# A Perceiver block on one core: VectorE and ScalarE in source order, with each step split in two

## Chip, cores and metric

The kernel runs on one core of a Trainium2 chip. The metric is the device time of one execution in microseconds (us); three runs of the kernel before are given, and one further execution was profiled. All arithmetic is in fp32.

The core's engines, as the profile names them: PE is TensorE (matrix multiplication; PEld is the loading of its stationary operand, which overlaps), DVE is VectorE, ACT is ScalarE, POOL is GpSimd, SP is the engine whose queue issues most of the DMAs. PE writes its products to PSUM, eight banks of 128 x 512 floats here; DVE and ACT read them from there.

## The reference

`x` is (4, 256, 256): four batches of 256 latents with 256 channels. `ctx` is (4, 4096, 192). Three residual stages follow each other, each on a normalised `x`:

```python
x = x + cross_attention(layernorm(x), ctx)     # 16 heads of 16, 4096 keys a batch
x = x + self_attention(layernorm(x))           # causal, 16 heads, q and k layernormed by head
x = x + slot_ffn(layernorm(x))
```

The slot network, for each batch, cut to its steps:

```python
h     = gelu(concat(x, slot_mean) @ w1 + b1)            # 256 x 128
logit = (h @ w2 + b2) / (abs(tau) + 0.1)                # 256 x 64 slots
alpha = softmax over the 8 largest logits, else 0       # routing
si    = (alpha.T @ x) / alpha.sum(tokens)               # slot inputs
gi, gh = si @ Wih.T + bih, S @ Whh.T + bhh
r, z  = sigmoid(i_r + h_r), sigmoid(i_z + h_z)
n     = tanh(i_n + r * h_n)
S_new = (1 - z) * n + z * S                             # gates
y     = S_new + attention among the 64 slots
out   = (alpha @ (layernorm(y) @ wvp + bvp)) @ wo + bo
```

## The kernel before

The function `fast_` (L914 to L1767) is what runs; an exact version stands behind a test on the softmax denominators (`in_range`, L1537, sets its condition) and isn't entered with these inputs.

**Rounds.** The cross-attention of a batch goes over its 4096 keys in 8 chunks of 512, and each chunk in two rounds, so there are 16 rounds `p` per batch `b`. The 8 PSUM banks are four pairs, `two[0]` to `two[3]`; a round calls them `w, x_, y, z` and the next round starts three pairs on. A round issues, in this order:

1. `cross_block` (L1617), the first of two: score matmuls (L183), 8 of them into each two pairs, and ScalarE's exps, two halves for the first pair (L1628) and whole pairs after (L1630);
2. `behind(w)`: the former round's `cross_weigh` (L1633), which multiplies its probabilities with the values (L197) into pair `w`; VectorE adds the result to the running sums (L1640, L1642), which frees the pair;
3. the second `cross_block`, into `x_, y, z, w`;
4. plan steps (below), into single banks of `x_` and `y`;
5. half of the next chunk's operands: keys in even rounds (`keys`, L92: matmuls L98 and L104, copies into `kt` by DVE L112 and ACT L113), values in odd ones (`values`, L119: matmuls L125 and L138, copies into `v` by DVE and ACT, L168). Each is split into `most()` and `rest()`, and the rest with the copies comes after the steps.

**Plan.** Everything behind the cross-attention of batch `b` is done as small steps in the rounds of batch `b+1`, from a table `plan[b, p, i]` (L1573 to L1607) with i = 0 or 2 ahead of the keys or values and 1 behind `most()`. In round 0 the sums are turned and divided (`cross_turn`, `turn` L207); round 1 projects (`cross_out`, L1248); rounds 2 to 4 make the self-attention's q, k and v (`qk`, L1266); an extra round 6 (`SELF_AT`) does its scores and exps (`self_block`, L1644) with the causal masks (L1668); round 7 turns the result, round 8 projects it (`self_out`, L1328); rounds 9 to 16 are the slot network: `hidden` (gelu, L1344), `routing` (L1349), `slot_inputs`, `gates` (L1419), `slot_qkv`, `slot_scores` (L1467), `at_turned` (L1478), `slot_mix` (L1483), `slot_values`, and `give` in round 5 of the batch after. The next batch's latents are loaded in round 2 (`load_x`, L993), normalised after round 8 (`normed_x`, L1003; `layernorm` L953), and made into queries in rounds 10 and 13. Weights that the steps share are made in the rounds of batch 0 by `set_...` functions.

After the fourth batch a fifth pass, b = 4, has only plan steps. To keep PE busy there, `fill` (L1044) issues idle matmuls at L1047, as many as the table `WAITS` gives in us, 0.43 us each.

**What sets the order.** PE is under a manual schedule in the main loop: it executes in source order. The order on DVE, ACT and POOL is chosen by the tile scheduler. Each engine executes its own instructions strictly in the order chosen, so an instruction that waits holds all behind it. Loads are issued by SP's queue, in order as well.

**Start.** The first latents are loaded, normalised and turned; the queries of batch 0 come first, then keys and values of chunk 0, then round 0.

## Time and profile before

| what | value |
|---|---|
| three runs | 934.31, 934.25, 930.0 us (median 934.25) |
| the profiled execution | 931.51 us, its span 929.7 us |
| ScalarE's large exps, L1630 | 384 times, 1045 ns each |
| score matmuls, L183 | 2048 instructions' worth in 282.8 us |
| weighing matmuls, L197 | 4096, 235.1 us |
| fill matmuls in the trace, L1047 | 162 records, 40.8 us |
| mean granted TensorE clock | 0.988 |

The page gives busy time by engine, the chain of work that ended last, and groups of instructions with their idle time and the operation that ended it (the "releaser"). A line of the timeline shows start, duration, engine, source line, operation, output and input, and in brackets how long the engine had been idle and who released it. "PEclk" is the share of the full clock that TensorE was granted. Matmul records can be missing to a few per cent, so counts in the page are below the program's.

Rounds without a step take some 10.5 us (batch 0: rounds begin at 50.94, 61.48 and 72.10), a batch from b = 1 on 17 rounds; the batches begin near 212, 425 and 640 us.

### The profile page before, as it was taken

The numbers are of one execution on the slowest core, as the hardware profiler recorded it, in microseconds if no ns is written. First come the engines' busy times: TensorE is split into PE (matmuls) and PEld (weight loads), VectorE is DVE, ScalarE is ACT, GpSimd is POOL, SyncE is SP. The second block draws the span as 40 slices with busy tenths as digits, with TensorE's granted clock in tenths as the row PEclk, the third lists the DMA queues.
The fourth block names the chain that finished last, engine by engine and source line by source line (L and its number), as shares of the span: only waits on it lengthen the run. The fifth ranks groups of instructions, "written<-read, shape, count | busy, mean of one in ns | idle before, by whom it ended". The sixth has DMA issues, their size and how long they took to land.

```text
span 929.7 us, 19031 instructions
## 1 busy us (share of the span) xinstructions
PE 880.1 (95%) x8171; PEld 471.4 (51%) x8171; DVE 331.1 (36%) x876; ACT 589.7 (63%) x833; POOL 45.1 (5%) x53
## 2 busy tenths in 40 slices
PE   8599999999999999999999999999999999999885
PEld 5244545544554545544554545545555455545563
DVE  5212222222444442322444243332344332224653
ACT  2477776757767677577666677667666777671320
POOL 1000100000002000000002010000001100000200
PEclk9799999999999999999999999999999999999997
DMA  6500101000000000000001000000001000000000
GB/s 181 136 24 24 35 24 47 24 24 24 23 24 24 24 5 20 24 24 24 24 24 35 2 24 24 24 24 24 24 23 36 2 24 24 1 2 1 12 1 17
DMA packets 21758, 25.72 MB, mean 28 GB/s; under 512 B 6496, under 2 KB 13216, under 8 KB 21664
## 3 DMA queue, kind: packets, MB, share of 16 engines
q1 hardware_dynamic: 20992, 23.88, 8.5%
q8 instruction: 66, 1.08, 0.5%
q10 hardware_dynamic: 576, 0.52, 0.2%
q14 instruction: 28, 0.23, 0.1%
q0 software_dynamic: 96, 0.01, 0.0%
HBM read 23.35 MB, written 1.05 MB: 26 GB/s over the span
## 4 chain that ended last, share of the span: by engine, by line
PE 84%; DVE 5%; ACT 5%; SPq 2%; DMA 2%; issue 1%; ACTq 0%; DVEq 0%
PE banks L183 28%; PE banks L197 25%; PE banks L990 6%; PE banks L98 6%; PE banks L125 5%; PE banks L104 3%; PE banks L138 3%; ACT prob L1630 3%; SPq L69 1%; PE banks L978 1%; PE banks L1682 1%; PE banks L1655 1%; PE banks L1047 1%; ACT prob L1665 1%; PE banks L212 1%
## 5 line engine op out<-in xcount | busy, mean ns | idle before, releaser
L1630 ACT ACTIVATE prob<-banks 128x1024 f32<-128x1024 f32 x384 | 367.5, 1045 | 12.0 <-PE banks L183 11.9
L183 PE MATMUL banks<-qh,kt 32*128 32x512 f32 x2048 | 282.8, 625 | 18.4 <-DVE kt L112 9.5
L197 PE MATMUL banks<-prob,v 128*32 128x256 f32 x4096 | 235.1, 381 | 3.9 <-ACT prob L1628 2.3
L1628 ACT ACTIVATE prob<-banks 128x512 f32<-128x512 f32 x256 | 139.0, 595 | 144.6 <-PE banks L183 144.4
L197 PEld LDWEIGHTS banks<-prob,v 128*32 128x32 f32 x4096 | 126.7, 110 | 129.6 <-ACT prob L1628 45.0
L183 PEld LDWEIGHTS banks<-qh,kt 32*128 32x128 f32 x2048 | 108.0, 184 | 146.3 <-issue 77.0
L1642 DVE TENSOR_TENSOR sums<-banks,sums 128x512 f32<-128x512 f32 x120 | 82.5, 691 | 215.0 <-PE banks L197 191.0
L125 PE MATMUL banks<-wv,ctx 128*128 128x256 f32 x256 | 62.5, 387 | 0.1
L98 PE MATMUL banks<-ctx,wk 128*128 128x512 f32 x128 | 61.7, 603 | 0.0
L125 PEld LDWEIGHTS banks<-wv,ctx 128*128 128x128 f32 x256 | 45.8, 190 | 13.0 <-ACT prob L1628 3.2
L113 ACT ACTIVATE kt<-banks,bk 128x512 f32<-128x512 f32 x32 | 22.0, 687 | 41.2 <-PE banks L104 41.0
L168 ACT COPY v<-banks 128x512 f32<-128x512 f32 x32 | 18.8, 587 | 45.1 <-PE banks L138 44.7
L1047 PE MATMUL banks<-idle 128*128 128x256 f32 x162 | 40.8, 398 | 2.9 <-DVE idle L1042 1.5
L112 DVE TENSOR_SCALAR kt<-banks,bk 128x512 f32<-128x512 f32 x32 | 24.0, 750 | 43.3 <-PE banks L104 42.9
L138 PE MATMUL banks<-wv,ctx 64*128 64x256 f32 x256 | 36.4, 401 | 0.0
L104 PE MATMUL banks<-ctx,wk 64*128 64x512 f32 x128 | 36.1, 641 | 0.0
L1665 ACT ACTIVATE prob<-banks 128x512 f32<-128x512 f32 (+1 forms) x40 | 23.9, 694 | 19.1 <-PE banks L1655 19.1
L168 DVE COPY v<-banks 128x512 f32<-128x512 f32 x32 | 21.9, 683 | 39.6 <-PE banks L138 39.6
L1047 PEld LDWEIGHTS banks<-idle 128*128 128x128 f32 x162 | 31.0, 199 | 8.6 <-ACT prob L1665 2.2
L1668 POOL TENSOR_TENSOR prob<-prob,tri 128x256 f32<-128x256 f32 x32 | 27.1, 866 | 166.1 <-ACT prob L1665 166.1
L98 PEld LDWEIGHTS banks<-ctx,wk 128*128 128x128 f32 x128 | 21.3, 190 | 19.3 <-ACT prob L1630 9.8
L1259 POOL TENSOR_TENSOR xo<-xo,abo 128x512 f32<-128x512 f32 x4 | 5.1, 1280 | 493.2 <-DVE tmp L965 493.2
(212 smaller groups left out, 578.8 us busy)
## 6 DMA issues: line engine op xcount, KB each, us to landing
ctx<-in_ctxT SPq DMA_DIRECT2D x32, 256.0 KB, 2.9
ctx<-in_ctxT SPq DMA_DIRECT2D x64, 128.0 KB, 3.1
x<-in_x SPq DMA_DIRECT2D x4, 256.0 KB, 3.9
out<-tmp SPq DMA_DIRECT2D x4, 256.0 KB, 2.5
wih<-in_ffn_WihT SPq DMA_DIRECT2D x1, 768.0 KB, 6.2
tmp<-in_ffn_WhhT SPq DMA_DIRECT2D x3, 256.0 KB, 4.7
wq<-in_L_xattn_Wq ACTq DMA_DIRECT2D x1, 256.0 KB, 4.1
wo<-in_L_xattn_Wo SPq DMA_DIRECT2D x1, 256.0 KB, 5.5
```

What stands on the lines that cost most here:

```text
L98: nc.tensor.matmul(pk[c], k.wk[:, 0, c * P : (c + 1) * P], cx[:, 0, :], start=True, stop=False)
L104: nc.tensor.matmul(pk[c], k.wk[left(c), 1, c * P : (c + 1) * P], cx[left(c), 1, :], start=False, stop=True,)
L125: nc.tensor.matmul(pv[n // 2][:, n % 2, :], cx[:, 0, n * P : (n + 1) * P], k.wv[:, 0, :], start=(n % 2 == 0), stop=False, skip_group_check ...
L138: nc.tensor.matmul(pv[u][:, i, :], cx[left(u), 1, n * P : (n + 1) * P], k.wv[left(u), 1, :], start=False, stop=True, skip_group_check=True,)
L168: copy(v[:, :, 0 : H * VW].rearrange("p i (h w) -> p i h w", w=VW)[:, :, :, 0:D], src.rearrange("p i (h d) -> p i h d", d=D),)
L183: nc.tensor.matmul(sc[:, m, :], kt[r, c, i * P : (i + 1) * P], qh[r, c, :], start=True, stop=True)
L197: nc.tensor.matmul(po[q * 32 : (q + 1) * 32, s * NQ : (s + 1) * NQ], v[:, i, w0 : w0 + 32], pr[s][:, m, e * NQ : (e + 1) * NQ], start=(fir ...
L990: nc.tensor.matmul(dst, lhs(c), rhs(c), start=(c == 0), stop=(c == 1))
L1047: nc.tensor.matmul(bank[:, 0:NQ], idle[:, 0:P], idle[:, 0:NQ], start=True, stop=True)
L1628: nc.scalar.activation(pt[:, m, :], sc[:, m, :], AF.Exp)
L1630: nc.scalar.activation(pt, sc, AF.Exp)
L1642: nc.vector.tensor_tensor(s.sums[c], po[:, c, :], s.sums[c], ALU.add)
```

## The change

- PE, DVE and ACT are put under the manual schedule, for the whole of `fast_`: each executes in source order. POOL and SP are as before.
- Steps become generators with one `yield`. What stands before it (it empties PSUM, as far as it can) runs at the step's place; what stands after runs once the round's `rest()`, with the `kt` or `v` copies, has been issued. Such a yield is put into `cross_out`, `qk`, `self_out`, `hidden`, `routing`, `gates`, `slot_scores` and `slot_values`.
- `load_x(1)` is issued right behind the second context chunk's load. The later loads stay in round 2 of the batch before.
- Start: keys' `most()` is issued before the queries, and the values of chunk 0 become the `behind` of round 0. The reduction `parity` and `pscale` come after the first layernorm.
- The two causal masks of a probability tile, one by POOL and one by DVE, become one DVE operation over both.
- `turn` takes the reciprocal straight from PSUM and copies the denominators after the multiplication. `gates` does the z part before the n part.
- Plan: `at_turned` moves from (14, 1) to (15, 0), `slot_mix` from (15, 2) to (16, 2), `slot_values` from (16, 0) to (5, 0) of the next batch, with `give` behind it at (5, 1). `in_range` is cut in two, at (9, 2) and (13, 1) of the last pass.
- `WAITS` and `SELF_WAIT` are lowered by eight fill matmuls in all.

```diff
-SELF_WAIT = 1.3
+SELF_WAIT = 0.86
 WAITS = {
-    0: (0.0, 1.3),
+    0: (0.0, 0.86),
...
-    6: (0.0, 3.0),
-    7: (0.0, 1.3),
+    6: (0.0, 2.2),
+    7: (0.0, 0.86),
...
-    12: (2.2, 0.0),
-    13: (0.4, 0.0),
-    14: (1.3, 0.0),
+    12: (1.7, 0.0),
+    13: (0.0, 0.0),
+    14: (0.86, 0.0),
...
-    nc.vector.tensor_copy(den, hd[:, :, :, D])
     rec = pool.tile([P, QT, 8], F32, name="rec", tag="rec")
-    nc.vector.reciprocal(rec, den)
+    nc.vector.reciprocal(rec, hd[:, :, :, D])
...
+    nc.vector.tensor_copy(den, hd[:, :, :, D])
...
-    with ExitStack() as es:
+    with ExitStack() as es, tc.manual_schedule(
+        engines={mybir.EngineType.PE, mybir.EngineType.DVE, mybir.EngineType.Activation}
+    ):
         return fast_(es, tc, nc, a, out, k, const, x0)
...
     cx1 = load_ctx(nc, a, cp, 0, 1)
+    batches[1].x = load_x(1)
...
         nc.vector.tensor_tensor(x1, halves(bank), s.xo, ALU.add)
+        yield
         s.x1n = halves(temp())
         layernorm(s.x1n, x1)
...
         nc.vector.tensor_tensor(s.x2, halves(bank), s.xo, ALU.add)
+        yield
         s.x2n = held.tile([P, QT, C], F32, name="x2n", tag="x2n", bufs=1)
         layernorm(s.x2n, s.x2)
...
         product(bank[:, 0:NQ], lambda c: w1[:, c, :], lambda c: s.x2nT[:, c, :])
+        yield
         s.hT = small.tile([DH, NQ], F32, name="hT", tag="hT", bufs=1)
         nc.scalar.activation(s.hT, bank[:, 0:NQ], AF.Gelu, bias=b1c)
...
+        yield
         for t in range(QT):
             nc.vector.max(best[:, t, :], lg[:, t, :])
...
-            ((14, 1), step(at_turned, s)),
-            ((15, 2), step(slot_mix, s)),
-            ((16, 0), step(slot_values, s)),
+            ((15, 0), step(at_turned, s)),
+            ((16, 2), step(slot_mix, s)),
...
-        plan[b + 2, 5, 0] = step(give, s)
-    plan[B, 13, 1] = in_range
+        plan[b + 2, 5, 0] = step(slot_values, s)
+        plan[b + 2, 5, 1] = step(give, s)
+    plan[B, 9, 2] = all_in_range
+    plan[B, 13, 1] = count_bad
...
-                for m in range(2):
-                    diag = pt[:, m, 0:n].rearrange("p (e q) -> p e q", e=2)[:, :, 0:P]
-                    (nc.vector if m else nc.gpsimd).tensor_tensor(
-                        diag, diag, tri.unsqueeze(1).to_broadcast([P, 2, P]), ALU.mult
-                    )
+                diag = pt[:, :, 0:n].rearrange("p m (e q) -> p m e q", e=2)[:, :, :, 0:P]
+                nc.vector.tensor_tensor(
+                    diag,
+                    diag,
+                    tri.unsqueeze(1).unsqueeze(1).to_broadcast([P, 2, 2, P]),
+                    ALU.mult,
+                )
...
+            def take(i, *room):
+                f = plan.get((b, p, i))
+                g = f and f(*room)
+                if g:
+                    next(g)
+                    late.append(g)
...
+            for g in late:
+                next(g, None)
```

## The prediction, before the result was known

> **What bounds the kernel now.** I read the page's busy shares first, then its chain of waits, then what TensorE waited for, then the stretches behind the long waits.

> ```profile
> PE 880.1 (95%) x8171; PEld 471.4 (51%) x8171; DVE 331.1 (36%) x876; ACT 589.7 (63%) x833; POOL 45.1 (5%) x53
> ...
> PE 84%; DVE 5%; ACT 5%; SPq 2%; DMA 2%; issue 1%; ACTq 0%; DVEq 0%
> ```

> TensorE is the bound. The change keeps its order and its count (but for eight fill matmuls), so it can win only from idle time of PE, the missing 5%, and from a lowered clock. The waits of PE by releaser:

> ```profile
> PE banks L183 <- DVE kt L112: 9.5, 1, 9.5
> PE banks L183 <- ACT prob L1665: 5.4, 3, 1.8
> PE banks L1479 <- DVE at L1476: 4.3, 3, 1.4
> PE banks L183 <- DVE v L168: 3.3, 5, 1.7
> ```

> One wait outweighs any other line; its stretch from the timeline (start, duration, what; in brackets the idle time before and who ended it), and then in 2 us windows (length, busy us of PE, PEld, DVE, ACT and POOL, granted clock, DMA share, GB/s):

> ```profile
> 32.04 0.59 SPq L995 DMA_DIRECT2D x<-in_x  x1
> 36.17 0.75 DVE L960 BATCH_NORM_STATS2 ln_st<-x 128x6 f32<-128x256 f32 x2 [7.67 <-DMA x<-in_x]
> 38.66 0.75 DVE L112 TENSOR_SCALAR kt<-banks,bk 128x512 f32<-128x512 f32 x1
> 39.46 2.09 PE L183 MATMUL banks<-qh,kt 32*128 32x512 f32 x8 [9.50 <-DVE kt L112]
> ```

> ```profile
> 30.00:32.00 2.00, 0.00 (x0) 0.00 (x0) 0.00 (x0) 1.98 (x3) 0.00 (x0) 1.00 0.46 46
> ...
> 40.00:42.00 2.00, 2.00 (x16) 0.29 (x12) 0.80 (x3) 0.39 (x1) 0.00 (x0) 0.50 0.00 0
> 42.00:44.00 2.00, 2.00 (x32) 0.98 (x28) 0.00 (x0) 1.55 (x2) 0.00 (x0) 0.71 0.00 0
> 44.00:46.00 2.00, 2.00 (x40) 0.97 (x36) 0.69 (x1) 0.00 (x0) 0.00 (x0) 1.00 0.00 0
> ```

> The scheduler put the layernorm of the second latents (L960) ahead of the key copy L112 on VectorE, and its data was issued at 32.04 and came at 36. So PE stood 9.5 us and then ran at half clock until 43.

> **The start: −13.** The load of x(1) moves ahead on SP's queue, behind the second context chunk; the layernorm goes to round 8. What is left in its place is the copy alone; next in PE's way there is the exp L1630 that it waited 0.33 for at 50.87. Round p=1 began at 28.82 and p=2 at 50.87: 22.05 us where the next rounds take 10.55 (61.48 less 50.94). That is 11.5 saved. The first key copy ran at 15.92 and 17.69 because queries (wq, then a wait on a weight) stood first; keys first and chunk 0's values in round 0 save about 1.5 more. −13, bounds −12 to −14: x(1)'s 256 KB now go ahead of the weights on SP's queue, and at the 265 GB/s seen at 32 to 34 that delays each by 1 us; the first reader of those, L1114's mean of wqkv, moves to p=4. If x(1) were late again, 11.5 is the price.

> **The rounds of a batch, three times (b=1 to 3).** In a round PE does scores, weighs the former round, more scores, plan steps, half of the next keys or values. A step's remainder now runs after the kt or v copies.
> - Gains. v copies behind statistics or a variance chain: L183 ×16 takes 2.4 for about 1.98 at p=1 and 3.48 for 1.95 at p=3, so −0.46 −1.45. at_turned goes a round later, off the wait at L1479: −1.4. Masks: 32 POOL and 32 VectorE operations (0.87 by the page, 0.56 to 0.72) become 32 VectorE ones of twice the width, 0.72 to 1.44; I take 1.1, twice 0.56. In the self round at 296 the last of POOL's ends at 299.41 (296.70+2.71), VectorE's at 298.82, and L1682 waits 0.76 for the former: −0.4. The longer mask runs beside ScalarE's exps L1665 (0.69); without that cover the last two a round would cost 2×0.4 more.
> - Hidden's gelu. Before, its table load came ahead of the copy:

> ```profile
> 545.76 1.28 ACT L1347 ACT_TABLE_LOAD   x1
> 547.41 0.47 ACT L1347 ACTIVATE hT<-banks,b1c 128x256 f32<-128x256 f32 x1 [0.36 <-PE banks L990]
> 548.50 0.69 ACT L113 ACTIVATE kt<-banks,bk 128x512 f32<-128x512 f32 x1 [0.62 <-PE banks L104]
> 549.21 1.28 ACT L1628 ACT_TABLE_LOAD   x1
> 550.50 1.09 ACT L1628 ACTIVATE prob<-banks 128x512 f32<-128x512 f32 x2
> 551.15 1.07 PE L197 MATMUL banks<-prob,v 128*32 128x256 f32 x16 [0.75 <-ACT prob L1628]
> ```

> Now: copy 0.69, load 1.28, gelu 0.47, load 1.28, then exps, which the weighing matmuls wait for: the first 1.28+0.47 come behind the copy, +1.75 and so +1.8 with a gap on PE of 0.75+1.75=2.5. Bounds 0 (the scheduler lifts the load) and 1.8; I take 1.8, nearest to the rows.
> - Routing. The six small activations L1376 (559.58 to 561.2) now follow the v copies and VectorE's top-8 chain, and still precede L1628's exps: the weighing begins 4.3 us after the scores for 2.87 before, +1.4, bounds 0 and 1.5.
> - Gates, z ahead of n: the matmul after it waits 0.2 to 0.5 longer: +0.5.
> - Sum of these: −0.46−1.45−1.4−0.4+1.8+1.4+0.5 = 0.0 a batch, bounds −3.2 and +0.5.

> **Two layernorms in a row.** At p=8 self_out's and the next batch's stand behind each other:

> ```profile
> 534.63 0.75 DVE L960 BATCH_NORM_STATS2 ln_st<-x 128x6 f32<-128x256 f32 x2
> ...
> 540.75 3.45 PE L183 MATMUL banks<-qh,kt 32*128 32x512 f32 x16
> 541.09 0.74 DVE L965 TENSOR_SCALAR tmp<-x,ln_mv,rs_y 128x256 f32<-128x256 f32 x2
> 541.74 1.28 DVE L1642 TENSOR_TENSOR sums<-banks,sums 128x512 f32<-128x512 f32 x2
> ```

> Interleaved they took 7.2 (534.63 to 541.83). One alone takes 4.1 to 4.3 (853.06 to 857.18 in the tail), two 8.6, and the v copies go ahead: the sums, which free the banks of the second block's scores, come 2.4 later in b=1 and b=2, with a gap on PE of up to 3.3. In b=3 there is no next batch: −0.5. Together +4.3, bounds −1.4 (only the copies gained) and +5.

> **The tail (b=4) and batch 0.** With no cross rounds PE runs fills and plan steps. Eight fills fewer save at most 8×0.43=3.4, and give back where the step behind them is late: VectorE's serial layernorm +0.2 twice, the second variance chain behind a copy +0.8, slot_values now in the last round +1.25, routing +0.3, against −1.4 in the self block and −0.6 in p=7 and p=14. With p=0's −0.3: about +0.6, bounds −3 and +3. Batch 0's set steps +0.5, bounds 0 and 1.

> **The sum without the clock.** −13 + 0.5 + 0.0 + 4.3 + 0.6 = −7.6.

> **The clock.** Gaps on PE lower it. In the self rounds PE waits 1.78 for L1665's exps, three times, and once the clock fell:

> ```profile
> 509.48 3.52 PE L183 MATMUL banks<-qh,kt 32*128 32x512 f32 x16 [1.79 <-ACT prob L1665]
> ```

> The window 510.78 to 514.19 had 0.50 granted: 3.41 us of half clock, work worth 1.7 lost, 1.65 with the edges. New gaps: gelu 2.5 and routing 2.2 three times each, p=9's up to 3.3 twice: eight. If each falls in the grid as its length over 3.41 (which makes the 1.78 gaps 0.52 each, one in three seen), that is 3×0.73+3×0.65+2×0.97 = 6, or +10. At the low end, gaps that are half as long as reckoned (they were added from durations in a row, with nothing of the preceding step let through), none. I take two windows, +3.3, since the row nearest in length, 1.78, cooled in one of three; bounds 0 and +13.

> [...]

> **The total.** −7.6+3.3=−4.3 on this execution's 931.5 (span 929.7) is 927.2. The runs' median, 934.25, lies 2.7 above it; I go some way towards it and say **928**.

> **Rivals.**
> 1. *The gaps cool the clock six or seven times* (+10 to +11 instead of +3.3): 931.5−7.6+10.5 = 934.4, no change. For it: the 1.79 gap that did it. Against: two of three like it didn't.
> 2. *The rounds win too.* If the gelu and routing remainders fall into slack (ScalarE is 63% busy, VectorE 36%), gelu and routing add nothing, the batches win 3.2×3=9.6 and p=8 wins 1.4: −13−9.6−1.4+0.5+0.6 = −22.9, so 908.6; midway to the forecast's −4.3, 918. Against: L1628's exps follow in order.
> 3. *Source order turns ScalarE into the gate of step rounds* (slower). ScalarE is not free to run exps while a remainder waits for VectorE; every round with a split remainder, seven a batch, 28 with the tail, would stand a further 0.7 beyond what I priced, the wait of L1628's releaser row (0.76), 28×0.7=20: 931.5−4.3+20 = 947. It decides from 0.42 a round (11.7 us, reaching 938.9). For it: ScalarE is the busiest engine beside PE. Against: most remainders are VectorE's alone.
> 4. *The start is not won*: x(1)'s load or the weights behind it delay chunk 1's work, and 8 of the 13 go: 936.

> **Chances.** About 0.5% (4.7 us) is what a measurement can tell from no change: faster is below 929.6, slower above 938.9. The forecast 0.45 (0.37 of it faster, 0.07 the same, 0.01 slower); the rounds win 0.17; cooled clock 0.15 (0.12 the same, 0.03 slower); start not won 0.04, the same; source order gates 0.19, slower. Faster 0.54, the same 0.23, slower 0.23. The forecast's own range is 921 to 934; with one in ten left on each side the range is 914 to 942.

> **What would show it.** The 9.5 wait at L183 gone and p=2 beginning near 38: the start right. L1347's load after L113, and L197 waiting 2.5 behind it: gelu right. L1642 at p=8 to 9 near 545, L183's ×16 over 5 there: layernorms right. Windows at 0.50 after these: the clock, counted at 1.65 each. A batch's period against 213.6 now (425 to 640, less the start) tells the rounds apart from the start. If the start's gain is under 10, or a batch's period moves over 4, the forecast is wrong.

## The result, and the profile after

Over twelve runs each, the kernel before has a median of 931.7 us (930.0 to 934.31) and the changed one 932.58 us (929.2 to 935.0). The ratio of the two is 1.0005, with a 95% interval of 0.9992 to 1.0018: no change that can be told from none. (The prediction's three runs had a median of 934.25; with twelve it lies at 931.7, and that is what the following differences are taken against.) The profiled execution after has a span of 931.7 us against 929.7.

The page after, first the busy times, then TensorE's granted clock in forty slices, and then the first lines of the view of TensorE's waits (time in all, how often, the longest):

```profile
PE 882.6 (95%) x8155; PEld 473.2 (51%) x8155; DVE 333.0 (36%) x876; ACT 590.1 (63%) x833; POOL 18.0 (2%) x21
...
PEclk9999999999999899999999989999999999999997
```

```profile
PE banks L197 <- ACT prob L1645: 8.9, 9, 2.0
PE banks L183 <- ACT prob L1682: 6.2, 3, 2.1
PE banks L183 <- DVE sums L1659: 5.0, 2, 2.5
PE banks L183 <- ACT hT L1356: 1.9, 3, 0.6
...
PE banks L183 <- DVE kt L112: 1.6, 1, 1.6
```

The shares by engine hardly differ, and yet the list of waits is another. The 9.5 us at the key copy L112 are gone, and the waits on L1479 and on the value copies L168 with them. In their place stand ScalarE's first exps (L1645, which was L1628; 8.9 us instead of 2.3) and VectorE's sums (L1659, which was L1642; 5.0).

So the start of each round was set side by side, from the first score matmuls of the round in either trace. The difference between them (after less before, in us) runs so:

| start of round | difference | start of round | difference |
|---|---|---|---|
| b=0, p=2 | −13.6 | b=2, p=9 | −8.2 |
| b=1, p=0 | −13.3 | b=2, p=11 | −0.7 |
| b=1, p=9 | −13.5 | b=3, p=9 | −2.2 |
| b=1, p=12 | −3.9 | b=3, p=12 | +1.2 |
| b=2, p=0 | −5.8 | b=3, p=16 | −0.2 |
| b=2, p=5 | −7.3 | end of the span | +2.0 |

The start wins 13.6 us. Rounds 9 to 11 of the three batches lose 21.5 together, the other rounds win 8.2 back, and the last pass loses 2.2. Two things in those rounds can be read from the timeline. First, round 9 of b=2, on VectorE and TensorE (start, duration, what, and in brackets the idle time and its releaser):

```profile
527.32 0.42 DVE L960 BATCH_NORM_STATS2 ln_st<-x 128x6 f32<-128x256 f32 x1
...
531.54 0.42 DVE L960 BATCH_NORM_STATS2 ln_st<-x 128x6 f32<-128x256 f32 x1
...
535.20 0.73 DVE L965 TENSOR_SCALAR tmp<-x,ln_mv,rs_y 128x256 f32<-128x256 f32 x2
535.85 1.28 DVE L1659 TENSOR_TENSOR sums<-banks,sums 128x512 f32<-128x512 f32 x2
536.59 1.72 PE L183 MATMUL banks<-qh,kt 32*128 32x512 f32 x4 [2.48 <-DVE sums L1659]
...
538.73 3.37 PE L98 MATMUL banks<-ctx,wk 128*128 128x512 f32 x4
```

Two layernorms stand one behind the other from 527.32 to 535.85, 8.5 us, and the sums behind them. The weighing had ended at 532.2, so the banks of the last score matmuls come free 2.5 us too late. Right after it, L98 takes 3.37 us for its four instructions, where the profile before has 1.88 at a granted clock of 1.00 (544.62): from 538.98 to 542.39 the granted clock is 0.50.

Second, round 10 of the same batch, on ScalarE and TensorE:

```profile
544.30 0.69 ACT L113 ACTIVATE kt<-banks,bk 128x512 f32<-128x512 f32 x1 [4.88 <-PE banks L104]
545.01 1.28 ACT L1356 ACT_TABLE_LOAD   x1
546.30 0.47 ACT L1356 ACTIVATE hT<-banks,b1c 128x256 f32<-128x256 f32 x1
546.79 1.28 ACT L1645 ACT_TABLE_LOAD   x1
546.83 1.12 PE L183 MATMUL banks<-qh,kt 32*128 32x512 f32 x2 [0.64 <-ACT hT L1356]
548.09 1.08 ACT L1645 ACTIVATE prob<-banks 128x512 f32<-128x512 f32 x2
548.74 3.65 PE L197 MATMUL banks<-prob,v 128*32 128x256 f32 x36 [0.79 <-ACT prob L1645]
```

The order on ScalarE is copy, load, gelu, load, exps. The gap on TensorE comes in two pieces, 0.64 and 0.79, because the gelu also holds a bank that the last two score matmuls need.

In the records of both profiles the granted clock is either 1.00 or 0.50, and the stretches at 0.50 can be read as windows (columns as in the prediction: stretch, length, busy us of PE, PEld, DVE, ACT, POOL, granted clock, DMA share, GB/s). These are all seven between the start and the tail's end in the profile after, of which one is a double one:

```profile
282.98:286.39 3.41, 3.41 (x16) 1.10 (x12) 0.77 (x2) 2.49 (x4) 0.00 (x0) 0.50 0.00 0
317.11:323.94 6.83, 6.27 (x12) 3.12 (x13) 1.80 (x3) 1.20 (x2) 0.00 (x0) 0.50 0.00 0
330.76:334.18 3.42, 3.31 (x32) 1.58 (x36) 0.00 (x0) 3.29 (x5) 0.00 (x0) 0.50 0.00 0
538.98:542.39 3.41, 3.41 (x6) 1.40 (x5) 0.69 (x1) 0.45 (x1) 0.00 (x0) 0.50 0.02 5
549.22:552.63 3.41, 3.41 (x40) 1.74 (x36) 0.56 (x1) 2.70 (x3) 0.00 (x0) 0.50 0.00 0
760.85:764.26 3.41, 3.37 (x32) 1.59 (x36) 0.00 (x0) 3.23 (x4) 0.00 (x0) 0.50 0.02 5
832.52:835.94 3.42, 3.42 (x16) 1.52 (x12) 0.00 (x0) 2.33 (x4) 0.00 (x0) 0.50 0.02 5
```

That is eight windows of 3.41 us. In this execution their starts are whole multiples of 3.413 us apart (317.11 less 282.98 is 34.13, ten of them; 832.52 less 282.98 is 549.54, 161 of them). Below, stretches at 1.00 are cut at these multiples as well and called windows too; that is a way of reading the profile, since the records show only where the clock changed. Before, the same part of the run had one (at 510.78). Seven more, at the 1.65 us each of the prediction, are 11.6 us; without them, by this estimate, the changed kernel's span would be 2.0−11.6=−9.6 against the one before. The count is that of one execution: its mean granted clock, 0.978, is that of seven of the twelve runs, and the other five had 0.983 or 0.985.

### The profile page after: what moved, and what is told of

Same layout as the page of the kernel before. It is cut to its first block, busy times and chain, and to the rows that moved or that the text cites. A ratio compares the mean times of both kernels' runs of the same rounds, so it can differ in the third digit from the quotient of the medians.

```text
span 931.7 us, 18962 instructions
## 1 busy us (share of the span) xinstructions
PE 882.6 (95%) x8155; PEld 473.2 (51%) x8155; DVE 333.0 (36%) x876; ACT 590.1 (63%) x833; POOL 18.0 (2%) x21
## 3 DMA queue, kind: packets, MB, share of 16 engines
q8 instruction: 66, 1.08, 0.5%
## 4 chain that ended last, share of the span: by engine, by line
PE 87%; DVE 6%; ACT 4%; issue 1%; ACTq 0%; DVEq 0%
PE banks L183 26%; PE banks L197 25%; PE banks L990 8%; PE banks L98 6%; PE banks L125 6%; PE banks L138 4%; PE banks L104 4%; PE banks L1048 2%; PE banks L978 1%; PE banks L1672 1%; PE banks L1701 1%; ACT prob L1647 1%; ACT prob L1682 1%; ACT prob L1645 1%; PE banks L212 1%
## 5 line engine op out<-in xcount | busy, mean ns | idle before, releaser
L183 PE MATMUL banks<-qh,kt 32*128 32x512 f32 x2048 | 279.7, 626 | 16.5 <-ACT prob L1682 6.2
L197 PE MATMUL banks<-prob,v 128*32 128x256 f32 x4096 | 239.2, 386 | 9.6 <-ACT prob L1645 8.9
L1645 ACT ACTIVATE prob<-banks 128x512 f32<-128x512 f32 x256 | 138.8, 594 | 140.4 <-PE banks L183 140.3
L197 PEld LDWEIGHTS banks<-prob,v 128*32 128x32 f32 x4096 | 128.2, 111 | 137.7 <-ACT prob L1645 54.3
L183 PEld LDWEIGHTS banks<-qh,kt 32*128 32x128 f32 x2048 | 108.4, 185 | 140.6 <-issue 74.0
L1659 DVE TENSOR_TENSOR sums<-banks,sums 128x512 f32<-128x512 f32 x120 | 82.2, 690 | 198.2 <-PE banks L197 180.0
L98 PE MATMUL banks<-ctx,wk 128*128 128x512 f32 x128 | 64.3, 626 | 0.1
L113 ACT ACTIVATE kt<-banks,bk 128x512 f32<-128x512 f32 x32 | 22.0, 687 | 47.5 <-PE banks L104 47.3
L168 ACT COPY v<-banks 128x512 f32<-128x512 f32 x32 | 18.7, 586 | 47.4 <-PE banks L138 46.8
L112 DVE TENSOR_SCALAR kt<-banks,bk 128x512 f32<-128x512 f32 x32 | 24.0, 750 | 54.0 <-PE banks L104 54.0
L168 DVE COPY v<-banks 128x512 f32<-128x512 f32 x32 | 22.1, 691 | 58.1 <-PE banks L138 57.9
L1048 PE MATMUL banks<-idle 128*128 128x256 f32 x146 | 38.1, 408 | 2.6 <-DVE idle L1043 1.5
L1682 ACT ACTIVATE prob<-banks 128x512 f32<-128x512 f32 (+1 forms) x40 | 23.9, 694 | 20.8 <-PE banks L1672 20.8
L104 PE MATMUL banks<-ctx,wk 64*128 64x512 f32 x128 | 36.1, 641 | 0.0
L98 PEld LDWEIGHTS banks<-ctx,wk 128*128 128x128 f32 x128 | 22.2, 197 | 20.5 <-ACT prob L1647 10.2
L1048 PEld LDWEIGHTS banks<-idle 128*128 128x128 f32 x146 | 28.6, 204 | 7.5 <-ACT prob L1682 1.9
L138 PEld LDWEIGHTS banks<-wv,ctx 64*128 64x128 f32 x256 | 22.6, 186 | 11.1 <-issue 9.6
L984 DVE COPY tmp<-banks 128x512 f32<-128x512 f32 x21 | 14.5, 692 | 35.4 <-PE banks L978 30.2
```

Of the source, the lines that this page charges most:

```text
L98: nc.tensor.matmul(pk[c], k.wk[:, 0, c * P : (c + 1) * P], cx[:, 0, :], start=True, stop=False)
L104: nc.tensor.matmul(pk[c], k.wk[left(c), 1, c * P : (c + 1) * P], cx[left(c), 1, :], start=False, stop=True,)
L138: nc.tensor.matmul(pv[u][:, i, :], cx[left(u), 1, n * P : (n + 1) * P], k.wv[left(u), 1, :], start=False, stop=True, skip_group_check=True,)
L168: copy(v[:, :, 0 : H * VW].rearrange("p i (h w) -> p i h w", w=VW)[:, :, :, 0:D], src.rearrange("p i (h d) -> p i h d", d=D),)
L183: nc.tensor.matmul(sc[:, m, :], kt[r, c, i * P : (i + 1) * P], qh[r, c, :], start=True, stop=True)
L197: nc.tensor.matmul(po[q * 32 : (q + 1) * 32, s * NQ : (s + 1) * NQ], v[:, i, w0 : w0 + 32], pr[s][:, m, e * NQ : (e + 1) * NQ], start=(fir ...
```

## The experiments

Each kernel ran beside the kernel before, on one chip; ratios are against that. Line numbers are of each kernel's own source, and differ by a few.

### The load alone

```diff
     cx1 = load_ctx(nc, a, cp, 0, 1)
+    batches[1].x = load_x(1)
...
-                if b + 1 < B and p == 2:
+                if 0 < b < B - 1 and p == 2:
```

This is in the kernel before, with the scheduler's order.

> The kernel before, with nothing changed but the place of the second latents' load (behind the second context chunk's, as in the changed kernel); the scheduler still orders VectorE and ScalarE. Theory (the start is worth 11.5 of the 13.5 us, and the rest of the change gives all of it back): the 9.5 us wait of L183 for the key copy falls to at most 3 (the layernorm may still stand ahead of the copy, but its data is there), and the time is 920 to 923. Rival (the gain at the start needs the source order): the wait stays above 6 us and the time is 928 or more.

Measured: 918.56 us, ratio 0.9856 (0.9839 to 0.9872). Round 2 of batch 0 starts 11.2 us earlier, and that difference stays within 0.9 us (after a half-clock window of its own at 286.8) until b=2, p=7, where the one half-clock window of before is met no more. The timeline of this kernel at the place of the old wait:

```profile
28.57 0.72 DVE L965 TENSOR_SCALAR tmp<-x,ln_mv,rs_y 128x256 f32<-128x256 f32 x2
29.21 0.74 DVE L112 TENSOR_SCALAR kt<-banks,bk 128x512 f32<-128x512 f32 x1
30.00 1.14 PE L183 MATMUL banks<-qh,kt 32*128 32x512 f32 x8 [1.10 <-DVE kt L112]
```

The layernorm's last operation (L965) still stands ahead of the copy, but its data is there, and 9.5 us of waiting are 1.1. The theory holds, and the time is 1.4 us below the better edge of its numbers. One moved load is worth 13 us, by itself; the rest of the change took all of it back.

### The gelu ahead of the copy again

```diff
         product(bank[:, 0:NQ], lambda c: w1[:, c, :], lambda c: s.x2nT[:, c, :])
-        yield
         s.hT = small.tile([DH, NQ], F32, name="hT", tag="hT", bufs=1)
```

> The changed kernel without the split in hidden: the gelu with its table load again stands ahead of ScalarE's key copy. Theory (the gelu's two table loads behind the copy hold the exps, and the gap cools the clock): rounds 10 of b=1 to 3 lose their 3.1 to 3.5 us each, with three half-clock windows fewer; 932.6 - 3x3.3 = 923, at least 926. Rival (in source order the wait only moves: the gelu now holds the key copy and so the scores): no more than 3 us are won, 930.

Measured: 918.96 us, ratio 0.9877 (0.9853 to 0.99). Round 10 is shorter by 3.4, 3.5 and 3.1 us in b=1 to 3. The half-clock windows after the gelu are gone, as are those at 283 and 833 in this execution. That round, in b=2:

```profile
538.58 0.47 ACT L1355 ACTIVATE hT<-banks,b1c 128x256 f32<-128x256 f32 x1 [2.56 <-PE banks L990]
539.67 0.69 ACT L113 ACTIVATE kt<-banks,bk 128x512 f32<-128x512 f32 x1 [0.62 <-PE banks L104]
540.38 1.28 ACT L1644 ACT_TABLE_LOAD   x1
541.67 1.09 ACT L1644 ACTIVATE prob<-banks 128x512 f32<-128x512 f32 x2
542.32 3.66 PE L197 MATMUL banks<-prob,v 128*32 128x256 f32 x64 [0.75 <-ACT prob L1644]
```

The gelu and its load lie ahead of the copy, in time in which ScalarE waited for TensorE anyway. The theory holds for the rounds (10.0 us), and the time is 4 us below the expected 923. Of the rest of the 13.6 us, 0.9 lie at the start, before the edit can act: the runs with this start began round 0 anywhere from 15.9 to 17.4 us. The remainder is half-clock windows in other places; whether they went by the edit or by chance is not shown.

### The next batch's layernorm one round later

```diff
-            if b + 1 < B and p == 8:
+            if b + 1 < B and p == 9:
                 normed_x(batches[b + 1])
```

> The changed kernel with the next batch's layernorm issued after round 9 instead of round 8. Theory (two layernorms in a row hold the sums of round 9's weighing, 5.0 and 4.0 us in b=1 and b=2, clock included): 932.6 - 9 + up to 1.5 for a wait in round 10 = 924 to 926. Rival (the layernorm is as much in the way in round 10, ahead of routing's step and the turned latents): 930 to 934.

Measured: 917.86 us, ratio 0.9853 (0.9837 to 0.9869). Round 9 takes 11.75 us in all of b=1 to 3 (18.6, 17.55 and 11.75 in the changed kernel), and round 10 is no longer for it. Round 9 of b=2:

```profile
521.44 0.74 DVE L965 TENSOR_SCALAR x2n<-x,ln_mv,rs_y 128x256 f32<-128x256 f32 x2
522.09 1.49 DVE L1659 TENSOR_TENSOR sums<-banks,sums 128x512 f32<-128x512 f32 x2
522.68 2.07 PE L183 MATMUL banks<-qh,kt 32*128 32x512 f32 x16
...
525.17 1.88 PE L98 MATMUL banks<-ctx,wk 128*128 128x512 f32 x4
```

The sums follow one layernorm, the sixteen score matmuls run through, and L98 takes 1.88 us for its four instructions, not 3.37. The two rounds of b=1 and b=2 win 12.6 us together, more than the 9 expected, because one layernorm is also better placed than the kernel before's two interleaved (13.6 us a round there). The time is 6 us below the expected 924. The gelu's windows are still there (three).

### No split at all

```diff
                 if g:
-                    next(g)
-                    late.append(g)
+                    for _ in g:
+                        pass
```

> The changed kernel in source order on all three engines, with every step issued whole, its remainder ahead of the key or value copies. Theory (the split helps layernorms and variance chains, and hurts gelu and routing): gelu and routing win back 3x3.3 and 3x1.1, but the copies stand behind layernorms of 4.3 us in rounds 1 and 8 and the variance chain in round 3, three times each, 2 to 4 us and often a half-clock window: 932.6 - 13 + 9x3 = 940 to 950. Rival (the split is worth little, the order is what counts): 920 to 932.

Measured: 954.97 us, ratio 1.0248 (1.0231 to 1.0265), above the expected range. Its first line in the view of TensorE's waits, and one of the twelve places:

```profile
PE banks L183 <- DVE v L168: 23.9, 12, 2.9
```

```profile
227.61 0.73 DVE L965 TENSOR_SCALAR tmp<-xo,ln_mv,rs_y 128x256 f32<-128x256 f32 x2
228.26 0.68 DVE L168 COPY v<-banks 128x512 f32<-128x512 f32 x1
229.00 2.08 PE L183 MATMUL banks<-qh,kt 32*128 32x512 f32 x6 [2.86 <-DVE v L168]
```

A value copy behind a whole layernorm stops TensorE for 2.9 us. So in source order the split is worth 22 us, and is needed for the long chains on VectorE; of the two splits that were taken out alone, only the gelu's is shown to cost. A kernel with the split and the scheduler's order was not run, so what the order is worth apart from the split stays open.

### Routing whole, and the slot steps and masks put back

```diff
             ALU.add,
         )
-        yield
         for t in range(QT):
             nc.vector.max(best[:, t, :], lg[:, t, :])
```

> The changed kernel without the split in routing: the top-8 chain and its six small exps stand ahead of the value copies again. Theory (routing's remainder behind the copies holds the exps by 1.1, 1.1 and 0.8 us in round 11 of b=1 to 3, and its gap of 2.0 us cools no clock): 932.6 - 3.0 = 929 to 930, with the windows at half clock as many as in the changed kernel. Rival (the copies now wait in its place, and the scores behind them): 932 to 934.

Measured: 933.56 us, ratio 1.0028 (1.0016 to 1.0041); the changed kernel has 1.0005. The gap that the split makes, in the changed kernel, and the place without the split:

```profile
563.23 1.06 ACT L1645 ACTIVATE prob<-banks 128x512 f32<-128x512 f32 x2
563.86 2.37 PE L197 MATMUL banks<-prob,v 128*32 128x256 f32 x40 [1.98 <-ACT prob L1645]
```

```profile
563.19 0.68 DVE L168 COPY v<-banks 128x512 f32<-128x512 f32 x1
563.92 1.13 PE L183 MATMUL banks<-qh,kt 32*128 32x512 f32 x6 [0.41 <-DVE v L168]
```

Round 11 wins 0.5, 0.5 and 0.8 us, and as much is lost elsewhere: that execution has four half-clock windows more, three of them after 830, which may be chance. It is also one of the four slowest of the ten (936.4 to 936.6 us); the other six took 932.5 to 933.7, and they too are no faster than the changed kernel. Of the 2.0 us gap 0.4 come back as a wait for the copies and the exps are late all the same: the rival's direction, at its number.

For the slot steps, `at_turned`, `slot_mix` and `slot_values` went back to the places that the kernel before has:

```diff
-            ((15, 0), step(at_turned, s)),
-            ((16, 2), step(slot_mix, s)),
+            ((14, 1), step(at_turned, s)),
+            ((15, 2), step(slot_mix, s)),
+            ((16, 0), step(slot_values, s)),
```

> The changed kernel with the slot steps' places as before: at_turned at (14,1), slot_mix at (15,2), slot_values at (16,0). Theory (the move is worth some 2.1 us from round 14 to the next batch and 1 in round 5, three times, and costs a gap of 1.9 us with a half-clock window in the last batch's round 15): 932.6 + 9 - 4 = 936 to 939. Rival (the steps weigh the same wherever they stand): 931 to 934.

Measured: 935.73 us, ratio 1.0037 (1.0023 to 1.0051). By round starts, rounds 14 to 16 together are 1.65 us longer in b=1 and b=2 and 1.2 in b=3, and round 5 is 0.8 shorter in b=2 and b=3; half-clock windows at 506 and 728, in the self rounds, come in, and the last pass is 5.4 shorter. In sum this kernel is 3 us slower (935.73−932.58), a little less than expected. But the trace has three half-clock windows more in the rounds (the third in round 9 of b=2), none of them in a round of the moved steps, and one less in the last pass, so what the moves themselves are worth is not settled.

For the masks, the two operations on POOL and VectorE returned:

```diff
-                diag = pt[:, :, 0:n].rearrange("p m (e q) -> p m e q", e=2)[:, :, :, 0:P]
-                nc.vector.tensor_tensor(
...
+                for m in range(2):
+                    diag = pt[:, m, 0:n].rearrange("p (e q) -> p e q", e=2)[:, :, 0:P]
+                    (nc.vector if m else nc.gpsimd).tensor_tensor(
```

> The changed kernel with the two masks of a tile by POOL and VectorE apart, as before. Theory (the single VectorE mask takes away a wait of 0.4 for POOL, four times): 932.6 + 1.5 = 934. Rival (the self round's gap on PE grew from 1.8 to 2.1 because of the longer masks; apart, the gap shrinks and the half-clock window at 283 goes): 929 to 931.

Measured: 932.98 us, ratio 1.0007 (0.9991 to 1.0022), and every round starts within 0.06 us of the changed kernel's, with the same half-clock windows. Neither theory nor rival: the masks are worth nothing either way.

### The mends together, and two attempts to go on

Gelu and routing whole, and the layernorm after round 9 (called the mended kernel below):

> The changed kernel with the three mends together: gelu and routing whole, the next batch's layernorm after round 9. Theory (the three losses are separate and add): -14.5 by the layernorm, -10 by the gelu, -3 by routing: 902 to 906. Rival (each mend uncovers the next wait, since the rounds are limited by ScalarE's order): 911 to 918.

Measured: 909.85 us, ratio 0.9776 (0.9737 to 0.9816); the single times are 906.39, 906.43, 913.26 and 913.67. The profiled one is of the first pair, and has one half-clock window ahead of the tail's end (806.7). By the rounds the mends add: in b=1 round 9 wins 6.8, round 10 3.1 and round 11 0.5; in b=2 it is 5.8, 3.2 and 0.5, and in b=3 3.1 and 0.8 (without round 9, where there is no second layernorm). The median is 4 us above the expected range because of the second pair. No trace of it was kept, but its mean granted clock is on record, 0.987 and 0.986 against 0.993: by estimate some 12 us more at half clock, three or four windows, which at 1.65 us each would be 5 to 6 of the 7 us. Against the load alone (918.56, ratio 0.9856) the mended kernel is some 9 us faster: so much the rest of the change is worth once its three losses are undone.

Then, on top of it, `slot_mix` of the last batch but one back to (15,2), since round 15 of the last batch has neither keys nor values to make and TensorE waits 1.88 us there:

```diff
-            ((16, 2), step(slot_mix, s)),
+            ((15 if b == B - 2 else 16, 2), step(slot_mix, s)),
```

> The mended kernel with slot_mix of the last batch but one at (15,2) as before, so that PE has work in round 15 of the last batch, which has no keys or values to make. Theory (the gap of 1.9 us there goes, and the half-clock window after it): 1.5 to 3 us less than the mended kernel, so 903 by its faster runs of 906.4. Rival (the step costs in round 15 what it wins): 906.

Measured: 909.01 us, ratio 0.975 (0.9728 to 0.9772). The gap went, another of 2.0 at L197 came, and the intervals overlap: no gain is shown. And with `give` in the self round:

```diff
-        plan[b + 2, 5, 1] = step(give, s)
+        plan[b + 2, 6, 1] = step(give, s)
```

> The same as best1, and give moved from round 5 into the self round 6, behind its second block. Theory (its matmuls fill part of the 2.1 us gap before round 7): round 6 gains up to what give takes, some 1 us, three times, and the last pass loses no more than 1: 901. Rival (give waits for a bank that the exps hold, and the scores of round 7 wait behind it): 903 to 906, no gain over best1.

Measured: 910.44 us, ratio 0.9761 (0.9733 to 0.9789). `give` itself waits 1.57 for the exps there. The rival was right in its cause and in that nothing is gained, though not in its time (903 to 906). These three are the fastest kernels of the study, and can't be told apart.

### Does a gap's length decide on the clock?

Routing's gap of 1.98 us cooled no window in the changed kernel (none was followed by a window at half clock, which is all that "cooled" says here), and the gelu's two pieces of 1.4 together cooled one in each of three batches (330.76, 549.22 and 760.85). Had length decided, it would have been the other way round. Read by windows, routing's gap lay across two each time, with at most 1.50 us of it in one (344.42, b=1), while the gelu's idle time fell into one (1.32 to 1.42 us). But with the gelu ahead, a whole routing gap of 1.87 us lay in one window (762.45) and cooled nothing. Two kernels put eight gaps of nearly the same length into rounds 3 to 10 of batch 0 of the mended kernel, at two different places:

```diff
+                if b == 0 and 3 <= p <= 10:
+                    for m in (2 * CHUNK, 2 * CHUNK, 256):
+                        nc.scalar.activation(spare[:, 0:m], spare[:, 0:m], AF.Exp, scale=0.0)
                 first = cross_block(s, i, kt, v, (w, x_, y, z))
```

> The mended kernel (layernorm after round 9, gelu and routing whole) with three idle exps (1024, 1024 and 256 elements, 2.4 us together) ahead of ScalarE's exps of the first block in rounds 3 to 10 of batch 0: eight gaps of some 2.0 us on PE, each after score matmuls and before weighing matmuls, as routing's gap was. Their results are used nowhere. [...] Rival (the gap's length alone decides, as the prediction had it, 2.0/3.41 = 0.6 a gap): 8x2.0 + 5x1.65 = 24 us more, four to six windows.

```diff
+            if c == 1 and s.slow:
+                for _ in range(4):
+                    nc.vector.tensor_copy(spare[:, 0 : 2 * NQ], po[:, c, :])
             if s.sums[c] is None:
```

> The mended kernel with four idle copies of the weighing's result (0.69 us each, used nowhere) ahead of VectorE's second sum in the same rounds 3 to 10 of batch 0: eight gaps of some 2.1 us on PE, each in the midst of the second block's score matmuls, where the two layernorms made theirs. [...] Rival (length alone): 8x2.1 + 5x1.65 = 25 us, with as many windows as in the run with ScalarE's gaps.

Measured: 924.92 us with ScalarE's idle exps and 938.67 us with VectorE's idle copies, where the mended kernel has 909.85. First the two windows of the former that hold a whole gap, then of the latter the four windows that stood ahead of a fall of the clock, and the first fall itself:

```profile
60.38:63.79 3.41, 1.71 (x20) 0.46 (x16) 0.36 (x1) 3.35 (x6) 0.00 (x0) 1.00 0.50 154
74.04:77.45 3.41, 1.60 (x28) 0.57 (x24) 0.00 (x0) 3.35 (x6) 0.00 (x0) 1.00 0.00 0
```

```profile
94.08:97.49 3.41, 1.69 (x15) 0.54 (x8) 3.13 (x7) 2.92 (x4) 0.00 (x0) 1.00 0.00 0
97.49:104.32 6.83, 6.83 (x12) 2.67 (x10) 0.42 (x1) 1.02 (x1) 2.48 (x2) 0.50 0.00 0
128.21:131.62 3.41, 2.33 (x11) 1.44 (x12) 0.87 (x2) 1.96 (x3) 0.00 (x0) 1.00 0.00 0
...
145.28:148.69 3.41, 2.83 (x13) 1.89 (x14) 0.70 (x3) 1.46 (x2) 0.00 (x0) 1.00 0.02 5
...
158.93:162.34 3.41, 1.68 (x11) 0.51 (x8) 2.85 (x5) 2.92 (x4) 0.00 (x0) 1.00 0.76 232
```

ScalarE's gaps are 1.70 to 1.81 us, between score and weighing matmuls: no window of the eight cooled, not even the one at 74.04 with 1.81 us idle. A window's end cut the other six gaps, and those windows held 0.7 to 1.5 us of idle time. The rounds lost 14.5 us by their starts, 1.8 each. VectorE's are 1.72 to 1.76, in the midst of score matmuls: four of eight cooled the clock, six windows in all (97.5 and 162.3 double, 131.6 and 148.7). Two of the falls came behind windows with 1.72 and 1.73 us idle; the other two came one window later, behind windows that were idle for only 1.08 and 0.58 us (128.21 and 145.28). Two gaps that lay in a window of score matmuls just as these, with 1.73 and 1.71 us idle (80.42 and 111.14), cooled nothing. Rounds 3 and 4, which met no window, lost 2.8 each; eight of these are 22.4 of 31.5 us, and 9.1 are left for six windows, 1.5 each.

So length alone doesn't decide, in one window or in all. That the place among the matmuls does is not shown either: the window at 60.38, which cooled nothing, had 1.56 of its 1.71 us of TensorE's work in score matmuls and 1.70 us idle, nearly what the two at 94.08 and 158.93 had. Nor did the clock fall after nearly every gap among score matmuls: it was four of eight. What decides stays open.

## Why the prediction was right and wrong

The range held the time. The likeliest case, 928 and faster, did not come about; its first rival did, no change with the clock cooled six or seven times, at 934.4. The step of the prediction that failed is "I take two windows, +3.3". There were seven more than before, 11.6 us. That the total is so near the first rival's is in part luck: without the clock the sum was 2.0 us better than reckoned (−9.6 for −7.6), and the clock 1 us dearer than the rival had it. The terms of the sum ahead of the clock were these, with what they measured:

| term | predicted | measured |
|---|---|---|
| start | −13 | −13.6 at round 2 |
| batch 0's set steps | +0.5 | +0.3 |
| v copies behind statistics (p=1), a batch | −0.46 | −0.45 |
| v copies behind the variance chain (p=3) | −1.45 | −1.04 |
| at_turned | −1.4 | −1.52 |
| slot_mix a round later | not priced | −2.0 +1.4 |
| slot_values in round 5 | not priced | +0.8 in b=2 and b=3 |
| gates | +0.5 | +0.27 |
| masks | −0.4 | 0 |
| gelu | +1.8 | +3.1 to +3.5, of it one window each |
| routing | +1.4 | +1.1, +1.1, +0.75, no window |
| two layernorms, b=1, b=2, b=3 | +2.4, +2.4, −0.5 | +5.0, +4.0, −0.5, of it two windows and one |
| tail | +0.6 | +2.2, of it about one window |
| sum without the clock | −7.6 | −9.6 |

The start was right, in its cause and its size: one late load behind a reordered instruction. The experiment with that load alone gave 11.2 us by round starts, where the prediction had priced it at 11.5.

The waits of the gelu and the layernorms were right in place and cause, and, with the windows taken out (1.65 each), in size: 1.5 to 1.8 for the gelu, 1.7 and 2.3 for the layernorms. Both edits that undo them gave their rounds back.

One small term was not there. The masks were priced by twice the 0.56 row; the double ones took 0.68 to 0.69 us (VectorE's single ones, read as 0.56 to 0.72, had taken 0.42 to 0.95), and the 0.4 us that POOL's lateness was said to cost did not show in any round start. The gates cost half of what was reckoned: their last activation stands behind the v copy, and the weighing of round 13 waits 0.20 us for the exps behind it, which the kernel before did not. The tail's terms as they are listed add up to some +0.45 without the fills (−2.95 if all of the fills' 3.4 counts), and not +0.6.

The clock failed in its choice and not in its arithmetic. The formula, a gap's length over 3.41, was the author's estimate, which no run bears out; it gave six, "or +10", and the text then set it aside for two by the one row in three of the self rounds. In number the six were close to what came. But it was right in part for the wrong reason: it charged routing's gaps, which never cooled, and charged the gelu's 2.5 us as one piece, when two pieces with 1.4 in all were followed by a window each time. Of the five gaps that the gelu and the layernorms made, all five cooled. The sixth and seventh windows that were not there before stand behind slot_mix's new place (832.52) and in the double one of b=1 (317.11); the one in the self round only moved from b=2 to b=1.

By the signs that the prediction set itself, p=2 began at 37.3 us (38 foretold), the gelu's load came behind the copy, and the sums behind both layernorms. But L197 waited 0.79 there and not 2.5, since 0.64 had gone to the score matmuls before it. And a batch's period, which was not to move by more than 4 us, rose by 7.5 from b=1 to b=2 and by 4.3 from b=2 to b=3: by this sign the forecast was wrong, although the time lay in its range.

The rival on the slower side, source order holding every step round by 0.7, did not come about in this kernel: outside rounds 9 to 11 no round is slower by more than 1.4 us, and most by nothing. Without the split it comes about, by VectorE and not by ScalarE.

## What to carry to other kernels

When TensorE is 95% busy, look for the single longest wait and mend it by its cause: here the load alone won 13 us, more than the whole change (ratio 1.0005). An order that is fixed by hand has to be checked for each remainder by what stands behind it on its engine: here long VectorE chains belonged behind the copies that TensorE waits for (23.9 us of waits where they stood ahead), a gelu with two table loads of 1.28 us ahead of them (10.0 us won in three rounds). And a gap on TensorE is priced with the clock it may cost: in the changed kernel the gelu's two pieces of 1.4 us together were followed by a half-clock window in each of three batches, by estimate 1.65 us more.
